# Squares, relu sums and statistics moved between the engines of a planned transformer layer, with a new plan

## The chip, the cores and the metric

The kernel runs on one core of a Trainium2 chip. The metric is the device time of one execution in microseconds (us), the median of three runs. The engines are PE (TensorE: matmuls; PEld is its weight load), DVE (VectorE), ACT (ScalarE), POOL (GpSimd) and SP (SyncE, which here only issues DMAs). PSUM has eight banks of 128x512 fp32, which the kernel hands out by itself.

## The reference, cut to what matters

The input is 4 batches of 1024 tokens with 128 features, all fp32. After a layer norm, two branches read the same normalised rows and are added to the input:

```
xn = layernorm(x)
q, k, v = split(xn @ W_attn + b_attn)             # 16 heads of 8 features
s = q k^T                                         # per head, 1024 x 1024
s = s - mean(s);  s = s / mean(|s|) * gain        # over the whole row, before the mask
r = max(where(causal, s, -1000), 0) ** 4
y = (r / (sum(r) + 1e-6)) @ v;  attn = y @ W_proj + b_proj
ffn = sum over the 2 best of 8 experts: weight * (silu(((xn w1 + b1)(xn w2 + b2)) wg + bg) w3 + b3)
out = x + attn + ffn
```

The attention is no softmax: a score goes through relu and is squared twice, and each row needs the mean of the absolute scores over all 1024 keys, masked or not.

## The kernel before

Everything is one graph of nodes. A node (`add(name, {engine: cost}, emit, deps, take, give, rank, ...)`) is a handful of instructions on one engine, with the buffers that it takes and gives back; where two engines are named, the plan chooses. `Plan.run` is a list scheduler that runs on the host when the program is built: it keeps a model time for each engine, and picks again and again the node that can start first, corrected by the hand-set tables `SOONER` (us by which a kind of node is preferred) and `RANK`. The order that it finds is the program order of each engine's queue, and each queue is in order on the chip. Where the plan sees PE idle inside an open accumulation it adds matmuls with zeros (L1450).

**Attention.** It goes by batch `b` (4) and chunk `c` of 512 queries (2), in `chunk`. Heads are taken four at a time: `r` (0 to 3) is a round, and the four heads of a round lie in four groups of 32 partitions, so that four matmuls of 32 rows or 32 columns run beside each other. Three PE streams run in each chunk:

- *up* (L948): the scores above the diagonal, wanted for mean(|s|) only. Each set fills four banks, and each bank is drained by an absolute sum (`abs`) on DVE (L961) or ACT (L963).
- *score* (L1072): the scores on and under the diagonal, keys in partitions and queries in columns, again four banks for a set. For `c == 1` and each `r` there are four sets `j` = 0 to 3 of 512 columns wholly under the diagonal, and then three on it (`diag`); for `c == 0` only the three. Each bank is made positive into `u1`: the diagonal part by a masked product on DVE (L1091), the rest by ACT (L1098) or DVE (L1100). Then two squares follow, each of two heads at once (up to 1024 columns), `u1` into `u` and `u` into itself, on ACT (L1123) or POOL (L1125).
- *av*: per set a values matmul (L1148, fourth powers against V) and a relu matmul (L1139, the relus against `pick`, one column of ones, which adds up the positive scores of a query; the mean of |s| is made out of that). Both go to one bank `acc` for each `r`.

After the last set of an `r`, `acc` is copied, turned (L1016) and normalised with small DVE and ACT instructions. After four `r`, the chunk's output is turned (L1189), the gate weights are turned (`wT`, L1198), both are projected (L1205, L1207), and DVE adds the result to `xt` (L1214).

**Start.** `norm` makes mean and variance for half a batch at a time: per 128 tokens a `bn_stats` (L473) and a `bn_aggr` (L474), then an addition (L475), a root on ACT (L491), a reciprocal and a product (L479, L480). `route` picks two experts for each token and gives each token and choice a row of `xs` in DRAM; 64 indirect DMAs on POOL (`scatter`, L725), 128 rows each, write the normalised rows there. Each scatter waits for the one before to land.

**Experts.** 36 tiles of 256 rows of `xs` (`experts`) start once the scatters and the weights have landed. Their matmuls (L1276, L1285, L1294) lie between those of the attention, by rank. Each tile ends in two indirect DMAs with addition on POOL (`give`, L1314) into `acc` in DRAM.

**End.** `collect` loads the experts' sums of each batch (L1405) after the last `give`, DVE adds them to `xt` chunk by chunk (L1414), each after the chunk's projection, and SP stores (L1419).

Of the kernel before, what the change touches and what calls it, by code (L numbers as in the profile page):

```python
# [16 lines left out]
P = 128  # L17
# [3 lines left out]
NH = 16  # L21
# [30 lines left out]
class Plan:  # L52
# [3 lines left out]
    HOP = 0.14  # L56
    LAG = {"PE": 0.2, "DVE": 0.085, "ACT": 0.1, "POOL": 0.045}

    SOONER = {"score": 0.41, "v": 0.2, "wT": -0.2, "kappa": -0.03, "gateT": 0.72, "abs": -0.01, "ys": -0.05, "stats": 0.02, "exp": 0.21, "sq": -0.43, "bound": 0.25, "proj": -0.38, "xg": -0.16, "give": 0.82, "yT": -0.45, "sum": 0.42, "heads": -0.15, "gate": -0.76, "headsT": 0.66, "normal": 0.07, "second": -0.74, "relu": 0.04, "y@DVE": 0.58, "relu@DVE": -0.11, "xT": 0.29, "xg@DVE": -0.06, "out": 0.72, "yT@DVE": 0.09, "gate@ACT": 0.47, "g": 0.26, "wT@ACT": 0.52, "mean": -0.26, "sq@ACT": -0.05, "warm": -0.05, "xg@ACT": -0.54, "up": 0.34, "q": -0.02, "blocks": -0.54, "spill": 1.02, "wT@DVE": -0.54, "gain": -0.18, "gates": -0.34, "av": -0.08, "yT@ACT": 0.1, "std": 0.08, "bound@ACT": 1, "scale": 5.03, "heads@ACT": 0.03, "h": 0.26, "q@ACT": -0.52, "reload": 0.77, "sq@POOL": -0.33, "rows": -0.76, "scatter": 0.76, "fill": 1.07, "q@DVE": -0.36, "xT@ACT": -0.2, "absq": 0.1, "hot": 0.31, "bias": -0.05, "turn": -0.03, "abs@ACT": -0.21}
    RANK = {"score": 46, "proj": 1, "yT": -1, "xg": 91, "sums": 10, "h": -28, "tbias": -18, "top": -2, "headsT": -14, "spill": 75, "blocks": 43, "place": 1, "sum": 102, "std": -101, "gateT": -140, "scatter": -43, "xT": -29, "y": -20, "exp": 15, "second": -12, "relu": -6, "mask": 15, "rows": 6, "scale": -200, "turn": -9, "wT": -2, "fill": 8, "ys": -7, "bias": -28, "g": 32, "give": -66, "gate": 22, "absq": 5, "norm": -7, "v": -12, "hot": -41, "stats": 9, "up": 96, "out": -199, "k": 242, "abs": 31, "weight": 33, "reload": 20, "sq": -164, "gain": 149, "kappa": 26, "heads": 17, "mean": 7, "q": -22, "av": 13}  # L60
    MODE = {"up": "rows", "score": "rows", "av": "columns", "gate": "columns", "heads": "columns"}

# [16 lines left out]
    def run(self):  # L79
# [9 lines left out]
        while len(order) < len(self.nodes):  # L89
            best = None  # L90
            for n in ready:
# [11 lines left out]
                for e, took in n.on.items():  # L103
                    s = max(start, at.get(e, 0.0))
                    if e == "PE":
                        s = max(start, at.get(e, 0.0) + self.turn(mode, self.MODE.get(n.name)))
# [10 lines left out]
            if e == "PE":  # L117
                mode = self.MODE.get(n.name)
# [47 lines left out]
def layer_kernel(  # L166
# [63 lines left out]
    def keep(shape, name, dtype=F32):  # L230
# [8 lines left out]
        "yT": (1, [P, CH]), "wT": (1, [P, P]), "asum": (2, [P, 2, CB, NH]), "shead": (2, [P, TB, NH]),  # L239
# [183 lines left out]
    own = keep([E, N_OWN], "own")  # L423
    one8 = keep([P, TB], "one8")
# [36 lines left out]
    def norm(b, rank, begin):  # L461
# [6 lines left out]
        for c in range(NC):  # L468
# [13 lines left out]
            def part(e, i0):  # L482
# [6 lines left out]
            n = add("stats", {"DVE": 1.7}, stats, rank=rank, begin=begin + 0.5 * c)  # L489
            n = add(  # L490
                "std", {"ACT": 0.15}, lambda e, here=here: nc.scalar.activation(s[:, here, 8], s[:, here, 8], AF.Sqrt), deps=[n],  # L491
                rank=rank,
            )
            n = add("std", {"DVE": 0.35}, invert, deps=[n], rank=rank)
# [56 lines left out]
        return cs  # L551

# [5 lines left out]
    def route(rank):  # L558
# [154 lines left out]
        for k in range(2):  # L713
            for b in range(B):
# [7 lines left out]
                for i in range(TB):  # L722
                    def scatter(e, k=k, b=b, i=i):
                        nn = b * TB + i
                        nc.gpsimd.indirect_dma_start(  # L725
                            out=xs, out_offset=bass.IndirectOffsetOnAxis(ap=slot[:, k * NTB + nn : k * NTB + nn + 1], axis=0),
                            in_=of_buf(xn[b])[:, i * WX : (i + 1) * WX], in_offset=None,
                        )

                    prev = add(  # L730
                        "scatter", {"POOL": 1.12}, scatter, deps=[prev, w, filled], rank=rank, after=1.55,
                        give=[xn[b]] if (k, i) == (1, TB - 1) else [],
                    )
                    dones[b].append(prev)
# [748 lines left out]
```

## Time and profile before

| What | us |
|---|---|
| median of 3 runs | 925.73 (922.01 to 926.84) |
| the profiled execution's own time | 921.4 |
| its span, first to last instruction | 919.7 |
| PE busy in the span | 886.8 |
| ACT busy | 808.4 |
| POOL busy | 674.6 |
| DVE busy | 599.5 |

The matmuls of *score* run through the eight chunks in order: batch 0 from 34 to 218 us (its second chunk from 102), batch 1 from 228 to 448, batch 2 from 466 to 696, batch 3 from 697 to 894. The second chunks of batches 1, 2 and 3 take 297 to 448, 542 to 696 and 769 to 894. The scatters run from 80.1 to 275.2 us, and the first expert tile starts at 289.0. All times are of the profiled execution, counted from the start of its span. A busy matmul time counts pipelined matmuls, so it is not work; a set of four matmuls appears as eight records, since each fp32 matmul is two instructions.

### The profile page before, as it was taken

Reading aid. Unit: us, or ns where it says so; the run is one execution under the profiler, and the core shown is the slowest. Engines: PE = TensorE matmul, PEld = TensorE weight load, DVE = VectorE, ACT = ScalarE, POOL = GpSimd, SP = SyncE. Lnnn points to the kernel's source line nnn. Section 1 sums busy time; section 2 is a strip of 40 time slices with the busy share of each in tenths; the row PEclk is TensorE's granted clock in tenths of the full one; section 3 lists DMA queues with packets and bytes.
Section 4 is the critical chain, followed back from the end, with each engine's and each line's share of the span. In section 5 each row is a group of like instructions: output and inputs, shape, how many; then the busy total and the mean of one; then the engine's idle time right before and its main releaser. Section 6 shows DMA issues by size and latency. Waiting matters only on the chain.

```text
span 919.7 us, 22396 instructions
## 1 busy us (share of the span) xinstructions
PE 886.8 (96%) x8013; PEld 479.5 (52%) x8013; DVE 599.5 (65%) x1579; ACT 808.4 (88%) x1925; POOL 674.6 (73%) x469
## 2 busy tenths in 40 slices
PE   7799999999998999999999999999999999999995
PEld 5346533333454655555666656544455566545452
DVE  7798856566786555666566757565567577656555
ACT  5889999999899989889887899799998988899993
POOL 4368888889777868777565773678787776788892
PEclk9799999999999999999999999999999999999998
DMA  4640000000005444553554354433222322232206
GB/s 109 240 155 13 25 22 21 21 25 22 24 22 158 108 118 108 124 136 93 143 136 124 87 132 107 109 76 81 76 71 75 74 66 65 72 80 64 63 9 189
DMA packets 92317, 79.19 MB, mean 86 GB/s; under 512 B 8431, under 2 KB 88366, under 8 KB 92206
## 3 DMA queue, kind: packets, MB, share of 16 engines
q1 hardware_dynamic: 79064, 68.50, 24.6%
q0 software_dynamic: 12416, 8.99, 6.8%
q8 instruction: 63, 1.03, 0.5%
q10 hardware_dynamic: 726, 0.27, 0.1%
q14 instruction: 48, 0.39, 0.1%
HBM read 58.13 MB, written 19.60 MB: 85 GB/s over the span
## 4 chain that ended last, share of the span: by engine, by line
PE 75%; ACT 9%; POOL 7%; DVE 5%; issue 2%; DMA 2%; ACTq 0%; DVEq 0%; POOLq 0%
PE bank L948 14%; PE bank L1072 14%; PE bank L1148 13%; PE bank L1139 8%; PE bank L1285 7%; PE bank L1276 7%; POOL u L1125 5%; PE bank L1294 4%; ACT bank L963 3%; ACT u L1123 3%; ACT u L1098 2%; POOL xs L725 2%; PE bank L1016 2%; PE bank L769 1%; PE bank L825 1%
## 5 line engine op out<-in xcount | busy, mean ns | idle before, releaser
L1125 POOL TENSOR_TENSOR u<-u 128x1024 f32<-128x1024 f32 (+1 forms) x280 | 503.5, 1863 | 125.2 <-ACT u L1098 40.8
L1123 ACT ACTIVATE u<-u 128x1024 f32<-128x1024 f32 (+1 forms) x360 | 339.3, 972 | 8.7 <-POOL u L1125 4.2
L961 DVE TENSOR_REDUCE asum<-bank 128x1 f32<-128x512 f32 (+3 forms) x418 | 205.3, 548 | 56.6 <-PE bank L948 56.1
L1098 ACT ACTIVATE u<-bank 128x512 f32<-128x512 f32 (+2 forms) x375 | 161.7, 498 | 41.0 <-PE bank L1072 24.5
L1072 PE MATMUL bank<-blk,blk 32*128 32x512 f32 (+3 forms) x1536 | 181.4, 527 | 3.9 <-DVE u L1091 2.6
L948 PE MATMUL bank<-blk,blk 32*128 32x512 f32 (+3 forms) x1536 | 184.1, 524 | 0.2
L963 ACT ACTIVATE bank<-bank 128x512 f32<-128x512 f32 (+3 forms) x350 | 169.7, 487 | 15.3 <-PE bank L948 13.2
L1091 DVE SCALAR_TENSOR_TENSOR u<-bank,causal 128x256 f32<-128x256 f32 (+1 forms) x384 | 119.9, 373 | 85.7 <-ACT u L1098 47.8
L1314 POOL DMA_INDIRECT acc<-ye,xg x72 | 113.4, 1576 | 70.7 <-DVE ye L1306 32.5
L1148 PE MATMUL bank<-u,V 128*32 128x512 f32 (+3 forms) x1536 | 162.0, 496 | 1.5 <-POOL u L1125 1.3
L948 PEld LDWEIGHTS bank<-blk,blk 32*128 32x128 f32 x1536 | 93.9, 185 | 75.3 <-DVE asum L961 11.8
L1139 PE MATMUL bank<-u,pick 128*32 128x512 f32 (+3 forms) x1280 | 126.9, 465 | 0.0
L1100 DVE TENSOR_SCALAR u<-bank 128x512 f32<-128x512 f32 (+1 forms) x137 | 87.1, 666 | 50.2 <-PE bank L1072 48.3
L1072 PEld LDWEIGHTS bank<-blk,blk 32*128 32x128 f32 x1536 | 68.9, 184 | 67.3 <-issue 19.7
L1139 PEld LDWEIGHTS bank<-u,pick 128*32 128x32 f32 x1280 | 43.2, 110 | 77.6 <-issue 74.5
L725 POOL DMA_INDIRECT xs<-blk,slot x64 | 63.6, 994 | 26.7 <-DMA xs<-blk,slot 17.7
L1148 PEld LDWEIGHTS bank<-u,V 128*32 128x32 f32 x1536 | 34.2, 108 | 90.7 <-issue 61.1
L1285 PEld LDWEIGHTS bank<-z,w 128*128 128x128 f32 x576 | 67.3, 191 | 19.4 <-DVE z L1360 5.5
L1285 PE MATMUL bank<-z,w 128*128 128x128 f32 x576 | 73.4, 281 | 0.6 <-DVE u L1091 0.6
L1360 DVE SCALAR_TENSOR_TENSOR z<-bank,biases,z 128x128 f32<-128x128 f32 x144 | 43.6, 345 | 42.1 <-ACT z L1353 30.7
L1276 PE MATMUL bank<-xT,w 128*128 128x128 f32 x576 | 70.3, 275 | 0.6 <-ACT u L1098 0.6
L963 ACT ACTIVATION_READ_ACCUMULATOR bank<-bank 128x1 f32 x350 | 68.2, 195 | 0.0
(175 smaller groups left out, 723.5 us busy)
## 6 DMA issues: line engine op xcount, KB each, us to landing
w<-in_L_ffn_w_dram SPq DMA_DIRECT2D x216, 128.0 KB
w<-in_L_ffn_wg_dram SPq DMA_DIRECT2D x72, 256.0 KB
xs<-w SPq DMA_DIRECT2D x1, 4680.0 KB
xg<-xs SPq DMA_DIRECT2D x36, 130.0 KB
acc<-w SPq DMA_DIRECT2D x1, 2048.0 KB
blk<-acc SPq DMA_DIRECT2D x4, 512.0 KB
out_dram<-xt SPq DMA_DIRECT2D x8, 256.0 KB
xt<-in_L_attn_x_dram SPq DMA_DIRECT2D x3, 512.0 KB
```

Of the source, the lines that this page charges most:

```text
L948: nc.tensor.matmul(of_buf(ks_[g])[:, at : at + w], of_buf(q[b])[rows_, ii * P : (ii + 1) * P], of_buf(km[b][r])[rows_, k0 : k0 + w], start ...
L961: nc.vector.tensor_reduce(to, of_, AX.X, ALU.add, apply_absolute_value=True)
L963: nc.scalar.activation(of_, of_, AF.Abs, accum_out=to)
L1072: nc.tensor.matmul(of_buf(ks_[g])[:, at : at + n], of_buf(km[b][r])[rows_, jj * P : (jj + 1) * P], of_buf(q[b])[rows_, c * CH + off : (c + ...
L1091: nc.vector.scalar_tensor_tensor(of_buf(u1)[:, g, :near], of_buf(k)[:, :near], 0.0, allowed[:, :near], ALU.max, ALU.mult)
L1098: nc.scalar.activation(to, s_, AF.Relu)
L1123: nc.scalar.activation(to, s_, AF.Square)
L1125: (nc.vector if e == "DVE" else nc.gpsimd).tensor_tensor(to, s_, s_, ALU.mult)
L1139: nc.tensor.matmul(of_buf(acc)[32 * g : 32 * g + 32, off + lo : CH], pick, of_buf(u1s[g // 2])[:, g % 2, at + lo : at + n], start=begin, s ...
L1148: nc.tensor.matmul(of_buf(acc)[32 * g : 32 * g + 32, off:CH], of_buf(Vb[b])[:, jj, h0 : h0 + 32], of_buf(us[g // 2])[:, g % 2, at : at + n ...
L1276: nc.tensor.matmul(of_buf(k)[:, m * TW + j * TS : m * TW + (j + 1) * TS], weights_of(i, j)[m][:, f * P : (f + 1) * P], of_buf(tile_[i]["xT ...
L1285: nc.tensor.matmul(of_buf(k)[:, g * TW + j * TS : g * TW + (j + 1) * TS], weights_of(i, j)[2][:, f, g * P : (g + 1) * P], of_buf(tile_[i][ ...
```

## The change

Seven things change; the seventh touches everything.

1. For the first batch, the first square of half the heads (`m == 0`, two of the four banks) is no longer made by ACT or POOL out of `u1`. DVE makes it out of the bank itself, max(score, 0) times `u1`, one bank at a time (`sqv`). The bank is given back after that.
2. From the second batch on, for `j` = 1 to 3 of the sets wholly under the diagonal, DVE adds max(score, 0) out of each bank to a sum in SBUF (`more`), starting from the relus of `j == 0`. One relu matmul set for each `r` takes the sum in place of four sets. The bank is given back when both `more` and the relu into `u1` are done.
3. The scatters no longer wait for each other (`apart`); each has a one-element memset on POOL ahead of it.
4. The statistics of batches 1 to 3 are made in one pass (`moments`): `bn_stats` for all 24 blocks of 128 tokens, then six instructions, one root and two instructions for all at once, in place of `bn_aggr` for each block and the rest for each half batch.
5. The gate weights are turned as soon as the chunk before has been projected, not after the chunk's own output was turned, and there are two buffers for them.
6. The experts' sums are added and stored at the end in another order: for the last chunk they are added to `xt` ahead of its projection's addition. The experts' ranks end at 0.93 of the planned span, before at 0.95.
7. The planner's constants are new: `HOP`, `SOONER`, `RANK` (with names of their own for batch 0 and the last chunk), some node costs, and `SPAN` 930 to 895. So the order of all queues is new.

The diff, cut to its core:

```diff
-    HOP = 0.14
+    HOP = 0.12
...
+    def moments(begins, rank):
...
+                for i in range(TB):
+                    nc.vector.bn_stats(stat[:, b, i, 0:6], xt[:, b * TB + i, :])
+            taken.append(add("moments", {"DVE": 2.05}, stats, rank=rank, begin=begins[b - 1]))
...
+        n = add("moments", {"DVE": 0.9}, merge, deps=taken, rank=rank)
+        n = add("moments", {"ACT": 0.15}, lambda e: nc.scalar.activation(v[:, :, 8], v[:, :, 8], AF.Sqrt), deps=[n], rank=rank)
+        return add("moments", {"DVE": 0.35}, invert, deps=[n], rank=rank)
...
+    def apart(d):
+        tc.add_to_no_dep_group("slots", d.ins)
+        tc.declare_no_dep(d.ins, group="slots", reason="no two rows go to one slot")
...
-                        nc.gpsimd.indirect_dma_start(
+                        nc.gpsimd.memset(scrap, 0.0)
+                        d = nc.gpsimd.indirect_dma_start(
...
+                        apart(d)
...
-                        "scatter", {"POOL": 1.12}, scatter, deps=[prev, w, filled], rank=rank, after=1.55,
+                        "scatter", {"POOL": 1.3}, scatter, deps=[prev, w, filled], rank=rank, after=0.3,
...
+        nth = b * NC + c
+            sums, added, relus_0 = [Buf("blk") for _ in range(2)], [], None
+            adds_up = nth >= NC
...
+                    direct = nth < NC and m == 0
...
+                            def product(e, w=w, g=g, k=k, u1=u1, u=u):
+                                nc.vector.scalar_tensor_tensor(
+                                    of_buf(u)[:, g, :w], of_buf(k)[:, :w], 0.0, of_buf(u1)[:, g, :w], ALU.max, ALU.mult
+                                )
+                            squared.append(
+                                add(
+                                    "sqv", {"DVE": t_dve(w)}, product, deps=parts_ + squared, take=[] if squared else [u], give=[k],
+                                    rank=rank - 100, behind=[] if squared else line["sq"],
+                                )
+                            )
...
+                if adds_up and not diag and j:
...
+                            def more(e, m=m, g=g, k=k, first=j == 1, before=relus_0, sums=sums):
+                                to = of_buf(sums[m])[:, g * CH : (g + 1) * CH]
+                                nc.vector.scalar_tensor_tensor(
+                                    to, of_buf(k), 0.0, of_buf(before[m])[:, g, :] if first else to, ALU.max, ALU.add
+                                )
+                            a = add(
+                                "more" + stage, {"DVE": t_dve(CH)}, more, deps=[scores] + (before_ if j == 1 else [added[2 * m + g]]),
...
+                            add("free", {"none": 0.0}, None, deps=[a, e1[2 * m + g]], give=[k])
...
+                    def all_relus(e, sums=sums, acc=acc):
+                        for g in range(4):
+                            nc.tensor.matmul(
+                                of_buf(acc)[32 * g : 32 * g + 32, :], pick, of_buf(sums[g // 2])[:, (g % 2) * CH : (g % 2 + 1) * CH],
+                                start=False, stop=False,
+                            )
+                    relu_job = None
+                    if j == c * CB - 1:
+                        relu_job = dict(acc=acc, emit=lambda e, f=all_relus: f(e), deps=list(added), took=took(CH), give=sums, free=None, last=None, take=[])
...
-        d = add("wT", {"PE": 0.2}, turnw, deps=[weighted[0], a], take=[kw, wT], rank=rank)
+        d = add("wT", {"PE": 0.2}, turnw, deps=[weighted[0]], take=[kw, wT], rank=rank - 15, begin=rank - 30, behind=last_projected)
...
+        final = b == B - 1 and c == NC - 1
+        first = [add_sums(b, c)] if final else []
...
-            deps=[a], give=[ko], rank=rank - 200,
+            deps=[a] + first, give=[ko], rank=rank - 200,
...
-    SPAN, BEGIN = 930.0, 25.0
+    SPAN, BEGIN = 895.0, 25.0
-    F0, F1 = 60.0, BEGIN + SPAN * 0.95
+    F0, F1 = 60.0, BEGIN + SPAN * 0.93
```

## The prediction

> **What bounds the kernel now.** I read the page's busy times first, then a table of stretches cut at the chunks, then the timeline of PE inside one stretch, then the groups by shape, then the waits and the tail.
>
> ```profile
> PE 886.8 (96%) x8013; PEld 479.5 (52%) x8013; DVE 599.5 (65%) x1579; ACT 808.4 (88%) x1925; POOL 674.6 (73%) x469
> ```
>
> Two engines are candidates, PE and ACT; DVE has 320 us free, and the change moves work onto DVE. The shares are means, so I cut them (length, then busy time of PE, PEld, DVE, ACT and POOL, with counts; then clock and DMA):
>
> ```profile
> 102.00:228.00 126.00, 124.14 (x1033) 49.60 (x1037) 80.27 (x189) 118.89 (x244) 112.55 (x85) 1.00 0.07 23
> 297.00:448.00 151.00, 149.97 (x1390) 85.88 (x1390) 89.78 (x233) 136.13 (x313) 109.50 (x64) 1.00 0.47 117
> 542.00:696.00 154.00, 153.83 (x1381) 82.79 (x1385) 94.50 (x235) 138.61 (x332) 109.92 (x65) 1.00 0.36 92
> 769.00:894.00 125.00, 125.00 (x1153) 63.55 (x1149) 75.16 (x190) 115.90 (x265) 103.92 (x60) 1.00 0.25 60
> ```
>
> The first is batch 0's second chunk, before any expert runs: ACT 94% and POOL 89% busy. The other three are the second chunks of batches 1 to 3: PE full, ACT 90%, 90% and 93%, DVE about 60%. The clock is full in all four.
>
> Is PE really full? The Trainium skill ("Perfetto Trace Analysis", Identifying the Most-Contended Engine) says that matmul busy time is no good measure of how near TensorE is to its limit, and tells one to take MFU and the weight-load share instead. The weight load is 52% busy, and by that PE would have room, and matmuls taken away would be worth next to nothing. So I looked at starts instead of busy times, in the second stretch of batch 2 (start, us, line, count):
>
> ```profile
> 662.81 1.14 PE L1072 MATMUL bank<-blk,blk 32*128 32x512 f32 x8
> 663.88 1.07 PE L1148 MATMUL bank<-u,V 128*32 128x512 f32 x8
> 664.77 0.61 PE L1139 MATMUL bank<-u,pick 128*32 128x256 f32 x8
> 665.31 1.15 PE L948 MATMUL bank<-blk,blk 32*128 32x384 f32 x16
> ```
>
> Each set begins when the one before must end: a 512-column set holds PE 0.89 us (663.88 to 664.77) between two sets of column tiles. PE streams without holes; I go with the row, against the rule. In batch 0 PE is only apparently full: the zero matmuls of L1450 fill 11.7 us of the stretch from 102 to 228.
>
> **The change part by part.** Durations:
>
> ```profile
> L1123 ACT ACTIVATE u<-u 128x1024 f32<-128x1024 f32 x284 | 295.5, 1063 | 6.1 <-POOL u L1125 4.0 <-DVE u L1100 0.7 <-DVE u L1091 0.4
> L1125 POOL TENSOR_TENSOR u<-u 128x1024 f32<-128x1024 f32 x228 | 449.3, 2030 | 116.1 <-ACT u L1098 40.8 <-DVE u L1091 37.4 <-DVE u L1100 29.9
> L1091 DVE SCALAR_TENSOR_TENSOR u<-bank,causal 128x256 f32<-128x256 f32 x256 | 91.5, 418 | 48.1 <-PE bank L1072 25.3 <-ACT u L1098 20.0 <-POOL u L1125 2.7
> L1214 DVE TENSOR_TENSOR xt<-bank,xt 128x512 f32<-128x512 f32 x8 | 5.5, 690 | 3.7 <-PE bank L1207 3.6
> ```
>
> *Relus added up.* Three batches, four rounds: four relu sets become one, so 36 sets go. 36 x 0.89 = 32 us of PE, all of it in stretches where PE is full. DVE gains 3 x 4 x 3 sets x 4 banks = 144 instructions with one input in PSUM and one in SBUF, like L1214: 144 x 0.69 = 99 us, 33 in each of the three stretches. Does it fit? Sum of DVE, ACT and POOL, with the 33, over three engines and a stretch shortened by 10.7: first (89.8 + 136.1 + 109.5 + 33) / (3 x 140.3) = 88%; second, the same way, 87%; third 328 / (3 x 114.3) = 96%. The highest such share now is the last stretch's, 79%. The plan can hand relus and absolute sums from ACT to DVE, so 88% I take as possible; 96% not, and I charge 5 us, half of that stretch's gain. In a DVE queue the `more` stand ahead of absolute sums and masks, and for those PE waits, by their banks; see the rivals.
>
> *Squares on DVE in batch 0.* Ten sets for each of four rounds, two banks each: 80 instructions, 64 of 512 columns and 16 of 256: 64 x 0.69 + 16 x 0.418 = 51 us on DVE. Gone are 40 squares, 32 of them of 1024 columns: about 39 us if ACT made them, 74 if POOL did (an estimate from 1.06 and 2.03 us, with 0.63 and 1.13 for the smaller). DVE has 46 us free in 102 to 228 alone. Behind each `sqv` stands whatever DVE does next, and each waits for a relu that may be ACT's.
>
> *Free scatters.* What they can win on POOL:
>
> ```profile
> POOL xs L725 <- DMA xs<-blk,slot: 17.7, 16, 1.9
> ```
>
> That is all: elsewhere POOL puts a square between two scatters (3.07 us from one to the next), and the landing is past by then. Each scatter gains a memset, 0.1 us by the small memsets at the start, and perhaps its own issue gap of 0.17: 64 x 0.1 to 0.27 = 6 to 17 us. So POOL gains 0 to 11 us by this. The experts' first load waits for all 64, so the experts start earlier by what batch 0 gains.
>
> What do these two bring at the end? The experts' matmuls come earlier, but PE is full from 290 on, so only PE time that is now empty in batch 0 counts: about 6 us of idle in 80 to 290, the zero matmuls (12), and 5.5 us idle in 25 to 80. Ends: 0 and 23 us. I take 8, a third, since PE must fit its work between drains there too.
>
> *Statistics.* A `bn_stats` with its `bn_aggr` takes 0.40 us in the start (10.08 to 10.50), alone some 0.29 (an estimate: the first's duration); 24 x 0.11, and eighteen small instructions become eight: about 4.5 us less on DVE before 27 us. Against it, batch 1's normalisation (ACT, 14.2 us) now waits for all three batches' statistics, to about 20. Ends: 4 gained, 4 lost; I take 2 gained, since the reduction for batch 0's bound stands in DVE's queue behind the last of these statistics, at 27.5 us.
>
> *Gate weights, sums, stores.* In DVE's tail the projection's addition waits behind three additions of sums:
>
> ```profile
> 908.39 2.56 DVE L1414 TENSOR_TENSOR xt<-blk,xt 128x512 f32<-128x512 f32 x4 [0.29 <-DMA blk<-acc]
> 911.23 2.02 DVE L1414 TENSOR_TENSOR xt<-blk,xt 128x512 f32<-128x512 f32 x3 [0.28 <-DMA blk<-acc]
> 913.16 0.69 DVE L1214 TENSOR_TENSOR xt<-bank,xt 128x512 f32<-128x512 f32 x1
> 913.88 0.69 DVE L1414 TENSOR_TENSOR xt<-blk,xt 128x512 f32<-128x512 f32 x1
> ```
>
> With the sums ahead, 1.4 us (913.16 less the matmuls' end at about 911.2, less a hop) and the last 0.7 go: 2. The weights' turn leaves the tail: 0.5. SP's stores and the sums' loads still wait for the last `give`; if the experts end late, all of the 2.5 is lost. I take 2.5.
>
> *The new order* has no row. It can cost or win anywhere; the sum holds it at 0, the range at 10 either way.
>
> **Sum**, against the profiled execution's 921.4: 921.4 - 32 + 5 - 8 - 2 - 2.5 = 881.9. The median of the runs shown is 0.47% above that execution (925.73 / 921.4), so 881.9 x 1.0047 = 886.
>
> **Rivals.**
>
> *All of batch 0's slack is won* (0.10): 23 us in place of 8: 871. For it: ACT and POOL carry a quarter less squaring. Against: DVE at 64% there gets 51 us more, and relus before `sqv` are a longer chain.
>
> *ACT, DVE and POOL become the bound in the second chunks* (0.14): if 88% can't be reached either, half to all of the 32 us is lost: 902 to 918, towards the upper end no change. For it: ACT is at 90 to 93% today, and most `more` wait for PE's scores, so DVE's free time isn't all where it is wanted. Against: over the stretches from 297 on, DVE has more free than it is given.
>
> *Banks held too long, slower* (0.08). A bank of scores is now given back after one relu; with ACT and DVE sharing four relus that is about 1.3 us after the scores. With four `more` on DVE the last comes 2.75 us after the scores, 4.1 if DVE makes two relus as well: 1.4 to 2.8 us longer for four of eight banks, one more being `acc`. If PE has nothing that it can do with the three left, each of 36 sets costs that: 50 to 100 us against some 40 gained: 935 to 985. It decides from 1.1 us lost on each set. Against: between two score sets of these stretches lie over 5 us (28 sets in 151 us), and an expert tile's matmuls need two or three banks.
>
> *POOL blocked by DVE.* In the Trainium skill ("SBUF — State Buffer", Who interferes with whom) a DVE instruction with two SBUF inputs shuts out a POOL instruction that reads SBUF. Were the 224 new ones of that kind, up to 150 us of POOL would stall, by an estimate from 0.69 us each, and the result would be slower. Their other input is PSUM; I give it nothing.
>
> **How the numbers follow.** The main case has 0.68, 872 to 900 by its own ends. Half a per cent (921.1 to 930.4) is about what a measurement of this kernel can tell from no change. Faster: 0.68 + 0.10 + 0.10 of the second rival = 0.88; the rest of that rival, 0.04, is no change; slower 0.08. The range, 866 to 914, leaves out the slow rival and the ends of the other two.
>
> **What would show it.** Relu matmul records (L1139's successor) fall by 288 and PE's busy time by over 30 us; `more` is a DVE group of 144 at about 0.69 us, `sqv` of 80; DVE is over 80% busy; the scatters end 15 to 40 us before 275; the tail has the projection's addition last. The argument is wrong if PE has holes in the second chunks that end on DVE instructions (rivals two and three), if `sqv` or `more` take over 0.8 us, or if batch 0's scores still end at 218.

## The result: 2.5% slower

| | before | after |
|---|---|---|
| median | 924.68 us (4 runs) | 947.09 us (945.53 to 951.3, 4 runs) |
| profiled execution, its span | 921.4, 919.7 us | 951.3, 949.6 us |
| mean granted clock | 0.988 | 0.967 |

The ratio is 1.0251 [1.0205, 1.0297]; 886 us were predicted, with a range up to 914. (The 925.73 of the front part is the median of three of the four runs.) Read first what came out as foreseen. From the page of the changed kernel, the busy times, and from its groups the relu sets by four (L1208), the sets that take the sums (L1256), the two forms of `more` (L1230) and `sqv` (L1166):

```profile
PE 892.9 (94%) x7739; PEld 501.3 (53%) x7739; DVE 687.4 (72%) x1677; ACT 788.7 (83%) x1962; POOL 738.7 (78%) x575
...
L1208 PE MATMUL bank<-u,pick 128*32 128x384 f32 (+3 forms) x896 | 73.1, 410 | 0.0
...
L1230 DVE SCALAR_TENSOR_TENSOR blk<-bank,blk 128x512 f32<-128x512 f32 x96 | 60.7, 683 | 14.8 <-ACT u L1147 14.5
L1166 DVE SCALAR_TENSOR_TENSOR u<-bank,u 128x512 f32<-128x512 f32 (+1 forms) x80 | 47.8, 627 | 0.0
...
L1230 DVE SCALAR_TENSOR_TENSOR blk<-bank,u 128x512 f32<-128x512 f32 x48 | 31.0, 686 | 20.8 <-ACT u L1147 18.1 <-PE bank L1119 2.6
...
L1256 PE MATMUL bank<-blk,pick 128*32 128x512 f32 x96 | 12.5, 592 | 0.0
```

The 1280 relu records (126.9 us busy) became 896 + 96 (85.6 us), the 144 additions cost 0.68 us each and the squares 0.69 us or less: the counts and durations of the prediction hold. DVE is 72% busy, not over 80%, and the last scatter starts at 227.9 us instead of 275.2, somewhat more than foreseen. Yet PE's busy time did not fall by 30 us; it rose by 6. Busy time of queued matmuls is not work, as the front part says. The `up` records, before and after:

```profile
L948 PE MATMUL bank<-blk,blk 32*128 32x512 f32 (+3 forms) x1536 | 184.1, 524 | 0.2
```

```profile
L992 PE MATMUL bank<-blk,blk 32*128 32x512 f32 (+3 forms) x1536 | 206.3, 541 | 1.7 <-ACT s L1497 0.7 <-DVE u L1140 0.3 <-ACT u L1147 0.3
```

Their busy time grew by 22 us and that of the `score` records by 18 (181.4 to 199.6), while the mean of one record hardly changed (524 to 541 ns, and 527 to 529). So the same records overlap less. I read this as waiting between the matmuls of a set; no run shows it directly. Where PE waits openly, the chain of releasers names two instructions for which PE had waited 1.8 us in all before (waits: waiting instruction, releaser, sum, times, longest):

```profile
ACT blk L890 <- DVE cstat L842: 22.1, 2, 12.5
...
PE bank L867 <- DVE kapB L849: 14.0, 1, 14.0
...
PE bank L867 <- ACT blk L890: 12.4, 1, 12.4
```

The windows of the changed kernel around these two places, the preparations of batches 2 and 3, with five microseconds out of the first of them ahead (length, busy PE, PEld, DVE, ACT, POOL, then clock), beside one of its second chunks:

```profile
450.00:455.00 5.00, 0.00 (x0) 0.00 (x0) 5.00 (x1) 0.00 (x0) 5.00 (x4) 0.50 0.01 4
...
444.00:464.00 20.00, 5.96 (x32) 2.18 (x26) 18.41 (x13) 4.94 (x10) 14.00 (x8) 0.66 0.10 23
682.00:702.00 20.00, 7.56 (x30) 3.16 (x28) 19.32 (x16) 6.59 (x12) 13.79 (x8) 0.66 0.11 24
...
550.00:682.00 132.00, 130.43 (x1117) 76.72 (x1110) 86.16 (x208) 116.67 (x295) 111.28 (x66) 1.00 0.39 97
```

PE is busy for 6 or 7.6 us in 20, ACT for 5 to 7. Only DVE and POOL are busy throughout, DVE with 13 and 16 instructions, and the granted clock falls to half. The timelines of these two engines at 444 us (start, us, engine, line) show what DVE is busy with:

```profile
444.45 13.57 DVE L841 TENSOR_TENSOR cstat<-cstat 128x1 f32<-128x1 f32 x1
458.06 0.23 DVE L842 TENSOR_SCALAR cstat<-rmask,cstat 128x4 f32<-128x4 f32 x1
```

```profile
444.45 13.55 POOL L1186 TENSOR_TENSOR u<-u 128x1024 f32<-128x1024 f32 x7
```

An addition of two numbers in each partition lasts 13.57 us. It begins with a run of seven squares on POOL and ends with it, to 0.02 us. Before the change the same instruction (L799 there) took 0.147 to 0.152 us in all four batches. It stood once more at 683.0, for 12.81 us. The code of this part was not changed. What changed is the order: it puts seven squares in a row on POOL just there (more on such rows in 5).

### The profile page after: what moved, and what is told of

It is laid out like the page before. It is cut to its first block, busy times and chain, and to the rows that moved or that the text cites. A ratio compares the mean times of both kernels' runs of the same rounds, so it can differ in the third digit from the quotient of the medians.

```text
span 949.6 us, 22138 instructions
## 1 busy us (share of the span) xinstructions
PE 892.9 (94%) x7739; PEld 501.3 (53%) x7739; DVE 687.4 (72%) x1677; ACT 788.7 (83%) x1962; POOL 738.7 (78%) x575
## 5 line engine op out<-in xcount | busy, mean ns | idle before, releaser
L1186 POOL TENSOR_TENSOR u<-u 128x1024 f32<-128x1024 f32 (+1 forms) x322 | 571.2, 1907 | 116.5 <-ACT u L1147 29.9
L1184 ACT ACTIVATE u<-u 128x1024 f32<-128x1024 f32 (+1 forms) x278 | 268.3, 994 | 7.8 <-DVE u L1140 2.8
L1147 ACT ACTIVATE u<-bank 128x512 f32<-128x512 f32 (+2 forms) x448 | 200.0, 520 | 63.3 <-PE bank L1119 30.9
L1005 DVE TENSOR_REDUCE asum<-bank 128x1 f32<-128x512 f32 (+3 forms) x386 | 190.8, 549 | 48.2 <-PE bank L992 47.1
L992 PE MATMUL bank<-blk,blk 32*128 32x512 f32 (+3 forms) x1536 | 206.3, 541 | 1.7 <-ACT s L1497 0.7
L1007 ACT ACTIVATE bank<-bank 128x512 f32<-128x512 f32 (+3 forms) x382 | 185.8, 490 | 19.8 <-PE bank L992 16.7
L1119 PE MATMUL bank<-blk,blk 32*128 32x512 f32 (+3 forms) x1536 | 199.6, 529 | 2.4 <-DVE u L1140 0.8
L992 PEld LDWEIGHTS bank<-blk,blk 32*128 32x128 f32 x1536 | 110.6, 190 | 75.8 <-ACT u L1147 11.0
L1119 PEld LDWEIGHTS bank<-blk,blk 32*128 32x128 f32 x1536 | 80.1, 184 | 68.1 <-issue 17.3
L1208 PE MATMUL bank<-u,pick 128*32 128x384 f32 (+3 forms) x896 | 73.1, 410 | 0.0
L1230 DVE SCALAR_TENSOR_TENSOR blk<-bank,blk 128x512 f32<-128x512 f32 x96 | 60.7, 683 | 14.8 <-ACT u L1147 14.5
L1387 PEld LDWEIGHTS bank<-xT,w 128*128 128x128 f32 x576 | 67.2, 192 | 0.8 <-DVE asum L1005 0.8
```

The lines of the kernel that those rows point to most:

```text
L992: nc.tensor.matmul(of_buf(ks_[g])[:, at : at + w], of_buf(q[b])[rows_, ii * P : (ii + 1) * P], of_buf(km[b][r])[rows_, k0 : k0 + w], start ...
L1005: nc.vector.tensor_reduce(to, of_, AX.X, ALU.add, apply_absolute_value=True)
L1007: nc.scalar.activation(of_, of_, AF.Abs, accum_out=to)
L1119: nc.tensor.matmul(of_buf(ks_[g])[:, at : at + n], of_buf(km[b][r])[rows_, jj * P : (jj + 1) * P], of_buf(q[b])[rows_, c * CH + off : (c + ...
L1147: nc.scalar.activation(to, s_, AF.Relu)
L1184: nc.scalar.activation(to, s_, AF.Square)
```

## The experiments

All ratios are to the kernel before, run on the same chip. The medians of the kernel before lay between 924.5 and 926.3 us. The edits are to the changed kernel where nothing else is said. A kernel called "replanned" has a new order of all queues; the others keep theirs.

**1. The form of the small addition.** Two SBUF inputs against one, and the same edit in the kernel before as a control.

```diff
-            nc.vector.tensor_tensor(mean, ks[:, 0:1], ks[:, 1:2], ALU.add)
+            nc.vector.tensor_reduce(mean, ks, AX.X, ALU.add)
```

> The changed kernel, with the mean of the keys (the 128x1 addition of two SBUF columns on DVE that took 13.6 and 12.8 us at 444 and 683) written as a reduction over the two columns, with one SBUF input. Nothing else changes, and all queues keep their order. Theory A, POOL's squares shut that addition out until POOL runs dry, and PE waits 14 and 12 us for what hangs on it: both stalls go, with the half clock after them; 947 falls by 25 to 42 us, to 905 to 922, and the reduction takes under 0.3 us. Theory B, banks are held too long by the additions out of PSUM and the preparation comes late for want of buffers: the holes at 446 to 460 and 686 to 698 stay, 940 to 950. Theory C, the three engines beside PE are overloaded in the second chunks: 935 to 948, since a hole is only the place where a backlog shows.

> The kernel before, with the same reduction in place of the addition, as a control. In its trace the addition took 0.15 us in all four places, so theory A, B and C all expect no change: 922 to 928. If it becomes faster, the reduction helps in some way other than by the stall.

Measured: 946.82 us, 1.0231 [1.0214, 1.0248], and 925.75, 0.9989 [0.9972, 1.0006]. No gain. The timelines of DVE and of POOL in the edited kernel say why:

```profile
439.67 13.54 DVE L842 TENSOR_SCALAR cstat<-rmask,cstat 128x4 f32<-128x4 f32 x1
```

```profile
439.62 13.55 POOL L1186 TENSOR_TENSOR u<-u 128x1024 f32<-128x1024 f32 x7
```

The reduction passed; the next instruction of the queue, a product with a scalar that takes 0.23 us elsewhere, stood in its place, and again at 678.5 for 12.85 us, also until the squares ended. So the shut-out is not bound to two SBUF inputs: a second form, SBUF to SBUF with a scalar from SBUF, is caught too.

**2. The three small instructions on ACT.** Order kept, in the changed kernel and, as a control, in the kernel before.

```diff
-            nc.vector.tensor_tensor(mean, ks[:, 0:1], ks[:, 1:2], ALU.add)
-            nc.vector.tensor_scalar(nkm, rmask, mean, -1.0 / T, ALU.mult, ALU.mult)
+            nc.scalar.activation(mean, ks[:, 0:1], AF.Identity, bias=ks[:, 1:2])
+            nc.scalar.activation(nkm, rneg, AF.Copy, scale=mean)
...
-            nc.vector.tensor_scalar(kapB[b % 2], same, kab, sign, ALU.mult, ALU.mult)
+            nc.scalar.activation(kapB[b % 2], signed, AF.Copy, scale=kab)
```

> The changed kernel, with all three instructions of the preparation that stood waiting on DVE taken to ACT, in the same places of the program: the addition of the two columns, the product with the row mask, and the 128x128 product for the bound (its sign multiplied in once at the start). With only the addition rewritten, the next instruction, the product with the row mask, stood 13.5 and 12.9 us in its place. Theory A (POOL's back-to-back squares shut out DVE instructions of some forms on SBUF): no form of that kind is left in the preparation; both holes of PE and the half clock after them go: 905 to 922. Theory D (DVE is held there by something else that lies behind these instructions, a semaphore or POOL's data): whatever stands there next waits as long, 940 to 950.

> The kernel before with the same three instructions on ACT. There the 128x128 product stood 1.6 to 2.0 us once, the others never. Theory A: gain of 0 to 3 us, or a loss of as much where ACT waits for DVE's reduction: 921 to 929. Theory D says the same.

Measured: 923.25 us, 0.9982 [0.9966, 0.9999], and 923.45, 0.9982 [0.9972, 0.9992]. The changed kernel gains 24 us, the kernel before 0.2%. ACT takes 0.29 to 0.41 us for each of them, and no stall is left. So the two stalls are the whole loss of the change, and without them it is no faster than before: of the forecast gain of 39 us some 38 are still missing. The rest of the runs look for those, from the changed kernel with this edit on, here called the kernel of 2.

**3. What the additions are worth.** No `more`, every relu set on PE; replanned. Once with the edit of 1, once with that of 2.

```diff
-            adds_up = nth >= NC
+            adds_up = False
```

> The changed kernel with the reduction, and without the relus added up by DVE: the 36 relu matmul sets are back on PE and 144 DVE instructions go; the plan is made anew with the same tables. Against the same kernel with them: if the additions won their 32 us of PE in part, this is 15 to 32 us slower (theory A, which leaves that step of the prediction alone). If they cost by held banks or DVE load (theories B and C), this is as fast or faster by up to 20 us.

> The changed kernel with those three on ACT and without the relus added up by DVE; the 36 relu matmul sets are back on PE. With the reduction alone this version took 935.2 with 7.3 us of a stall left. If the additions win their PE time once no stall is in the way: 12 to 32 us slower than with them. If they win nothing since ACT, POOL and DVE are the bound there: within 8 us.

Measured: 935.2 us, 1.0106 [1.0087, 1.0125], and 929.27, 1.0046 [1.0033, 1.0058]. The first run still has a stall of its own (7.35 us), so the second is the one to read. Against 923.25 the additions seem to bring 6 us of the predicted 27, but not where they were to bring them. From the last score of batch 0 to the last score of all, where the second chunks lie, it takes 673.0 us with the additions (231.1 to 904.1) and 674.7 without (229.7 to 904.4). Behind the last score, where no addition runs, it takes 17.5 us with them and 23.0 without, a difference between the two orders. So the additions win about 2 us.

**4. Why so little.** The prediction counted DVE's time and, as a rival, the bank that is held longer. The timelines of ACT and DVE in the kernel of 2 show a third thing, how the relu and the addition of the same four banks lie:

```profile
353.54 2.06 ACT L1151 ACTIVATE u<-bank 128x512 f32<-128x512 f32 x4 [1.20 <-PE bank L1123]
```

```profile
354.18 2.48 DVE L1234 SCALAR_TENSOR_TENSOR blk<-bank,blk 128x512 f32<-128x512 f32 x4 [1.19 <-ACT u L1151]
```

Both read the bank and neither needs the other's result. Yet DVE, idle for 1.19 us, begins only when the first relu has ended, 0.64 us after its start, and the waits name ACT:

```profile
DVE blk L1230 <- ACT u L1147: 32.7, 38, 2.1
...
ACT u L1147 <- DVE blk L1230: 12.9, 18, 1.0
```

(These two lines are of the changed kernel; each engine waits for the other.) In this program two engines do not read one bank at once: one waits for the other's semaphore. So a bank is held for relu plus addition, 0.64 + 0.68 us here, where the two were thought to run side by side. Two runs in the same order shorten either half. In the first the additions make 64 of 512 columns; in the second the relus of these banks do, and the squares read what the buffers held before. Both leave out that work, and their times are read for the holding alone.

```diff
-                                    to, of_buf(k), 0.0, of_buf(before[m])[:, g, :] if first else to, ALU.max, ALU.add
+                                    to[:, :64], of_buf(k)[:, :64], 0.0, of_buf(before[m])[:, g, :64] if first else to[:, :64], ALU.max, ALU.add
```

> The kernel with the three instructions on ACT (923.3), each of the 144 additions of relus cut to 64 of its 512 columns and emitted in the same place, so that all queues keep their order; the sums of relus left out are wrong by that. In that kernel the second chunks of batches 1 to 3 run 6 us each behind the order's own times, without the additions they don't. Theory E: two engines read one bank after the other (the addition on DVE waits for the relu on ACT of the same bank, in 38 places for 32.7 us), so each bank of scores is held by relu plus addition; a short addition frees the bank 0.5 us sooner: 10 to 25 us faster, 898 to 913. Theory F: DVE has too much to do: faster by as much, for its load falls by 75 us. Theory G: the loss lies elsewhere (sums, acc, the one late relu matmul): within 5 us.

```diff
+                        def relu(..., part_=bool(adds_up and j and not diag)):
-                            s_, to = of_buf(k)[:, near:w], of_buf(u1)[:, g, near:w]
+                            e_ = near + 64 if part_ else w
+                            s_, to = of_buf(k)[:, near:e_], of_buf(u1)[:, g, near:e_]
```

> The same kernel with full additions, and the relus of the same 144 banks cut to 64 columns, again in the same order; the squares behind them read stale columns. Theory E (bank held by relu, then addition): the bank comes free 0.4 us sooner and DVE waits less for ACT: 8 to 25 us faster. Theory F (DVE's own load): DVE's work does not change: within 5 us, or a little more from the relus that DVE makes itself. Theory G: within 5 us.

Measured: 911.54 us, 0.9854 [0.9833, 0.9875], and 912.15, 0.9867 [0.9847, 0.9888]. In the first, the second chunks of batches 1 to 3 take 151.0, 148.7 and 128.3 us, against 158.5, 155.8 and 134.3 in the kernel of 2: 20.6 us less. In the second it is 19 less. The chunk of batch 1 as windows, of the kernel of 2, of the first run and of the second, with the same 1290 matmul records:

```profile
306.00:464.50 158.50, 153.56 (x1290) 88.28 (x1290) 103.07 (x246) 140.04 (x348) 137.49 (x79) 1.00 0.38 91
```

```profile
315.70:466.70 151.00, 148.77 (x1290) 86.58 (x1290) 83.77 (x246) 139.51 (x347) 137.40 (x79) 1.00 0.39 95
```

```profile
314.50:466.80 152.30, 149.78 (x1290) 87.40 (x1290) 102.56 (x246) 123.52 (x348) 137.19 (x79) 1.00 0.39 94
```

The first run relieves DVE (103.1 to 83.8 us) and leaves ACT as it was; the second relieves ACT (140.0 to 123.5) and leaves DVE. Both gain nearly the same, so neither engine's load explains both gains; the bank, which both runs free sooner, explains them. Since both leave work out, the 20 us are an upper bound for the holding alone. With the bank freed sooner, the stretch from the last score of batch 0 to the last of all takes 652.3 and 653.5 us, against 676.1 before and 673.0 in the kernel of 2. So most of the predicted 27 us is there once the bank is free.

In both runs batch 0 ended later than in the kernel of 2 (scores to 240.8 instead of 231.1 in the first, to 239.6 in the second), although nothing there was edited. I have no cause for that; it hides part of the gain in the whole time.

**5. Free the bank, pay in SBUF.** The additions that follow the relu of their bank in the program (100 of 144) read the relu in SBUF; order kept. This frees the bank early with the work left whole, and is the way that the change did not take.

```diff
-                                    to, of_buf(k), 0.0, ...
+                                    to, of_buf(u1s[m])[:, g, :] if (id(u1s[m]), g) in made else of_buf(k), 0.0, ...
```

> The kernel with the three small instructions on ACT (923.25) in its own order; the additions that follow the relu of their bank in the program read that relu from SBUF instead of the bank, so the bank is free after the relu alone. If the bank held through relu and addition one behind the other is what costs some 19 us of the second chunks: 904 to 912. If the load of the additions on VectorE is what costs: no change, 920 to 926. These additions have two SBUF inputs, as the small addition that stood for 13.57 us beside GpSimd's squares: if such inputs are shut out by each square, an addition waits for the next gap of GpSimd, the sums come late, and it is slower than 930.

Measured: 1048.3 us, 1.1346 [1.1308, 1.1383], 125 us slower than without the edit. Its groups, additions from SBUF, squares on POOL, and the additions still from PSUM:

```profile
L1192 POOL TENSOR_TENSOR u<-u 128x1024 f32<-128x1024 f32 (+1 forms) x322 | 582.3, 1925 | 145.0 <-ACT u L1153 38.4 <-ACT u L1190 30.3 <-DVE u L1145 29.5
...
L1236 DVE SCALAR_TENSOR_TENSOR blk<-u,blk 128x512 f32<-128x512 f32 x71 | 125.1, 1809 | 15.2 <-ACT u L1153 15.2
L1236 DVE SCALAR_TENSOR_TENSOR blk<-u,u 128x512 f32<-128x512 f32 x29 | 52.3, 1810 | 16.5 <-ACT u L1153 16.5
...
L1236 DVE SCALAR_TENSOR_TENSOR blk<-bank,blk 128x512 f32<-128x512 f32 x25 | 15.8, 678 | 0.6 <-PE bank L1124 0.6
```

With two SBUF inputs the addition takes 1.81 us in the mean, with one 0.68. The mean hides two kinds. The same two groups by their shortest, median and longest, in ns:

```profile
L1236 DVE SCALAR_TENSOR_TENSOR blk<-u,blk x71: 674/693/14484, 313.1 to 1007.0; 128x512 f32<-128x512 f32 x71
L1236 DVE SCALAR_TENSOR_TENSOR blk<-u,u x29: 674/1270/7465, 307.2 to 1000.7; 128x512 f32<-128x512 f32 x29
```

At least half of the larger group run at full speed, and a few stand for up to 14.48 us; the 100 lose 113 us together. How long one stands depends on the squares beside it. Two rows of seven squares of this run, and the row of the changed kernel at 444 us, with the shortest, median and longest square and the starts of the first and last:

```profile
L1192 POOL TENSOR_TENSOR u<-u x7: 1888/2336/2337, 306.2 to 319.5; 128x1024 f32<-128x1024 f32 x7
```

```profile
L1192 POOL TENSOR_TENSOR u<-u x7: 2446/2466/2487, 484.4 to 495.5; 128x1024 f32<-128x1024 f32 x7
```

```profile
L1186 POOL TENSOR_TENSOR u<-u x7: 2443/2463/2486, 444.5 to 455.6; 128x1024 f32<-128x1024 f32 x7
```

In the first row no record overlaps the next. An addition gets in after each of the first six squares, having waited for one at most, and the squares from the second on take 2.34 us instead of 1.89. In the other two a square starts every 1.85 us but is recorded with 2.44 to 2.49, so that each begins before the one before has ended. There DVE gets nothing in: one addition stood 14.48 us to the end of the second row. Beside squares recorded with 2.40 us or less no addition of this run took over 2.41 us. All seven rows that held a DVE instruction for 10 us or more, in the changed kernel, in that of 1 and in this one, begin before the record of an indirect DMA on POOL has ended. Whether that makes the second kind was not tried. Both kinds say why an input in PSUM was a sound choice.

**6. Squares on DVE in batch 0.** First without them (replanned, with the edit of 1 and with that of 2), then only in the second chunk (replanned), then in the same order with 64 columns, where the second square reads the relus, so that the first square is left out there, on every engine.

```diff
-                    direct = nth < NC and m == 0
+                    direct = False
```

> The changed kernel with the reduction, and without the squares out of PSUM in batch 0: 40 squares are back on ACT and POOL. Batch 0's scores ended at 231 us in the changed kernel and at 218 before, so the squares on DVE may have cost 12 us rather than won 8. If they do: 5 to 15 us faster than with them. If they win and the loss in batch 0 has another cause (the new order, DVE's queue): 5 to 20 us slower, and scores of batch 0 end later than 231.

> The changed kernel with those three on ACT and without the squares out of PSUM in batch 0. With the reduction alone it took 961.7, with stalls of 3.0 and 9.2 us left and additions of sums at the end that took 2.4 us in place of 0.7. If these squares win time of their own: 10 to 35 us slower than with them. If what it lost is the stalls and the end: within 8 us.

```diff
-                    direct = nth < NC and m == 0
+                    direct = nth == 1 and m == 0
```

> The kernel with the three on ACT, and the squares out of PSUM only in batch 0's second chunk, planned anew with the same tables. DVE is 92% busy from 31 to 85 us there, with the routing and the preparation, and ACT only 64% from 55 to 85. If those first squares on DVE are what makes batch 0 late: its scores end before 222 in place of 231, and the whole by -10 to +5 us, as the order behind is another. If batch 0's lateness is the order itself: the end of its scores stays at 228 to 234.

```diff
-                                    of_buf(u)[:, g, :w], of_buf(k)[:, :w], 0.0, of_buf(u1)[:, g, :w], ALU.max, ALU.mult
+                                    of_buf(u)[:, g, :64], of_buf(k)[:, :64], 0.0, of_buf(u1)[:, g, :64], ALU.max, ALU.mult
...
-                        lambda e, ...: square(e, w, u, u), deps=a
+                        lambda e, ...: square(e, w, u1 if direct else u, u), deps=a
```

> The kernel with the three small instructions on ACT (923.25) in its own order; the squares on VectorE in batch 0 make 64 columns, and the second square of these heads reads the relus, so that the first square is left out of the result there. If VectorE's load by these squares (and the bank held through them) is what makes batch 0 end 13 us later than in the kernel before: batch 0's scores end at 218 to 222 in place of 231, whole kernel 911 to 916. If it is the new order or the statistics, nothing: 921 to 925.

Measured: 961.69 us, 1.0378 [1.0357, 1.0399]; 944.4, 1.0204 [1.0168, 1.024]; 939.25, 1.0161 [1.014, 1.0181]; and 918.58, 0.9933 [0.9907, 0.9959]. The three replanned kernels can't be read for the squares. In the third, batch 0's scores do end earlier, at 220.3 instead of 231.1, and yet the whole is 16 us longer, all behind batch 0, where nothing was edited but the order. The last run keeps the order: with the load of the squares gone, batch 0's scores end at 226.9 and the kernel gains 4.7 us. So the work itself costs batch 0 about 4 us. What the squares would cost there on ACT and POOL, in the same order, was not tried, so the worth of moving them stays open. The other 8.5 of the 12.7 by which its scores end later than before (231.1 against 218.4) come with the new order. The start of batch 0, before and then in the changed kernel:

```profile
31.00:102.00 71.00, 67.08 (x593) 36.16 (x595) 58.84 (x156) 61.64 (x153) 49.67 (x37) 0.94 0.33 121
```

```profile
31.00:102.00 71.00, 64.62 (x532) 38.34 (x530) 64.87 (x165) 55.06 (x136) 45.43 (x52) 0.90 0.35 129
```

Fewer matmuls, squares and ACT instructions lie in the same 71 us, the clock is lower, and DVE is 91% busy. Here it is short of time; the mean of 65% hid it.

**7. The scatters.** Waiting again, in the new order; and free, in the old order (an edit to the kernel before).

```diff
-                        apart(d)
```

> The kernel with the three on ACT, the scatters waiting for each other again, the memsets kept, the same order. In the changed kernel groups of two to eight scatters follow each other 1.3 us apart; each would then wait for the landing, about 2.3 us: some 40 such pairs by 1.0 to 1.3 us are 40 to 50 us of POOL in 72 to 228. If POOL is on the path of batch 0: 10 to 40 us slower. If scatters have room (theory of the prediction: 0 to 11 us on POOL): 0 to 8 us slower.

```diff
+                        nc.gpsimd.memset(scrap, 0.0)
-                        nc.gpsimd.indirect_dma_start(
+                        d = nc.gpsimd.indirect_dma_start(
...
+                        apart(d)
```

> The kernel before in its own order, with one edit: the scatters do not wait for each other and each has the one-element memset ahead of it. The prediction gave this part 0 to 11 us on GpSimd, which was idle 17.7 us for it: 914 to 926. If the 32 us that the same waits cost in the changed order were its worth in any order, it is 895 to 905. If the 64 memsets and scatters that run closer together hold up other work of GpSimd, 927 or more.

Measured: 953.49 us, 1.0316 [1.0282, 1.0349], and 916.79, 0.9919 [0.9891, 0.9948]. In the new order the waits cost 30 us, in the old one 7.7. The waits of POOL in the first run, and the scatter group of the second:

```profile
POOL xs L769 <- DMA xs<-blk,slot: 52.6, 34, 2.5
```

```profile
L733 POOL DMA_INDIRECT xs<-blk,slot x64 | 63.6, 994 | 11.8 <-issue 9.9 <-POOL scrap L732 1.6 <-PE bank L1157 0.3
```

The new order puts scatters close behind each other, so there the landing is waited for 34 times instead of 16, and batch 0's scores end at 261.0 instead of 231.1. The price of a wait belongs to an order. The second run is the fastest kernel of this study with the work left whole, 0.8% ahead of the kernel before, by one edit of the seven and no new plan. (The run of 8, which has the same edit and ran on another chip, is 0.4% ahead.)

**8. The tail.** The last sums ahead of the projection's addition, on top of the free scatters of 7 (before_free); old order up to the last microseconds.

```diff
+        first = [add_sums(b, c)] if final else []
...
-            deps=[a], give=[ko], rank=rank - 200,
+            deps=[a] + first, give=[ko], rank=rank - 200,
```

> before_free (916.79) with the sixth part of the change alone: the experts' sums of the last chunk are added ahead of its projection's addition, the experts' ranks left at 0.95; the order is the old one up to the last microseconds. The prediction gave this end 2.5 us: 913 to 916. If the 7.7 us by which the changed kernel's end is shorter come from it: 908 to 911. If they come from the order in which the last experts lie between the last scores, and not from the sums: 916 to 918, no change.

Measured: 922.49 us, 0.9962 [0.995, 0.9974]. From the last score to the end it takes 25.4 us, with 25.3 in before_free and 25.2 before: the order of the sums alone wins nothing. The 7.7 us that the changed kernel's tail is shorter (17.5 us) come from elsewhere in the new order of the last work; which part of it was not tried. Nor is it known why this run lies 0.4% above before_free. So the free scatters are worth 0.4 to 0.8% in the old order. The statistics, the gate weights and the planner's constants were not run alone.

## Why the prediction was wrong

Stretch by stretch, in us of the profiled executions, with the difference to before:

| | before | predicted | kernel of 2, no stalls | additions cut to 64 columns (4) |
|---|---|---|---|---|
| to the last score of batch 0 | 218.4 | -10 | 231.1 (+12.7) | 240.8 |
| from there to the last score | 676.1 | -27 | 673.0 (-3.1) | 652.3 (-23.8) |
| behind it | 25.2 | -2.5 | 17.5 (-7.7) | 17.5 |

The changed kernel adds its two stalls, 24 us, to the kernel of 2. (Of the 10 us predicted in the first row, 8 are for squares and scatters and could also be won in the second.)

**Relus added up: -32 and 5 back, measured -2 to -3.** The count (288 records gone) and the additions' duration held. The step that failed is the fit: the three engines' busy times were added up (88%) as if a relu and an addition could lie beside each other. They exclude each other at the bank, and about 20 us of the second chunks went there (4). The Trainium skill ("PSUM — Partial Sum Buffer", PSUM bank collisions raise a hardware error) says that two engines must be kept apart at a bank by semaphores, since the chip does not hold one back. The 32.7 and 12.9 us of waits are that discipline in the trace. Rival three had the right place, banks held too long. Its size was off: it asked for 1.4 to 2.8 us lost at each of 36 sets and called 1.1 the point of decision. Measured is 20.6 / 36 = 0.57 at most, so alone it would have left a small gain.

**POOL blocked by DVE: 0, measured +24.** This step made the kernel slower where it would have been the same. The prediction asked whether the 224 *new* instructions could shut out POOL. It had the wrong set and the wrong direction: old instructions, with all operands in SBUF and 0.15 and 0.23 us long, were shut out *by* POOL, and only the new order brought them beside such a row of squares. The rule of the Trainium skill ("SBUF — State Buffer", Who interferes with whom) was at hand. It names two SBUF inputs as a case, and `tensor_scalar` as an operation that can enter it, and says that who issues first keeps the ports for the whole instruction. The traces agree on both forms (L841, and L842 in run 1) and differs on the length: by the rule a loser waits out one square, 1.9 us; here it waited out seven, 13.6 us. Run 5 shows both, the wait for one square and the wait for all seven, and what goes with each; why was not tried. The rest is a chain: ACT's keys and PE's bound wait for DVE's number, no score can start, and the granted clock falls to half (0.66 in the mean of each 20 us).

**Squares and scatters: -8, measured +12.7 in batch 0.** The scatters alone won 3.8 to 7.7 us in the old order (8, 7), within the 0 to 11 that they were given on POOL. The squares were placed by DVE's mean load, and batch 0's start has none to give (6): their work costs about 4 us there. The other 8.5 us came with the new order.

**Statistics: -2; tail: -2.5, measured -7.7.** The scores begin at 31.4 us in the kernel of 2 and at 34.1 before, which fits the first, but no run isolates it. That the tail shrank was luck: the named cause wins nothing (8).

**The new order: 0, range 10 either way.** It is no single term. It brought the stalls (24 us), the 8.5 us of batch 0 and the shorter tail, and it set the price of the scatters' waits (30 us against 7.7). Terms measured in different orders do not add up, and what in the order makes batch 0 late stays open. The three replanned kernels of 6 agree in kind: an edit inside batch 0 costs 15 to 21 us against its own starting point (946.82 or 923.25) after a new plan with tables set for another graph.

## What to carry to other kernels

Before an operation is given to a second engine, look at what the two share besides time: here they shared the PSUM bank, and free DVE time bought 2 or 3 us where 27 were expected. After any change of order, list the instructions whose duration has grown against their own kind; a 0.15 us instruction that lasts 13.6 us is seen at once in the minimum and maximum of its tile, and in no busy share. And try each part of a large change alone in the old order: here one part of seven won 0.4 to 0.8%, while the whole lost 2.5%.

## What was not expected of the hardware

A run of POOL squares kept a DVE instruction with SBUF operands waiting to its very end: 13.57 us for seven squares, 12.81 us in the next batch, 10.8 us beside five. There POOL pays nothing visible: a square starts every 1.85 us. But not every row of squares does this. Where the records of the squares did not overlap (5), DVE got in after six of seven, and POOL slowed down too, from 1.89 to 2.34 us a square. A pause of POOL lets DVE in too. Before the change a single square stood at the same place, with nothing behind it on POOL until 694.71 us, and the addition ran right after its end at 688.80 (timelines of DVE and POOL of the kernel before):

```profile
688.81 0.15 DVE L799 TENSOR_TENSOR cstat<-cstat 128x1 f32<-128x1 f32 x1
```

```profile
686.32 2.48 POOL L1125 TENSOR_TENSOR u<-u 128x1024 f32<-128x1024 f32 x1
```

Not every small instruction is caught: a `tensor_scalar` of one column (L806) ran in its 0.15 us at 688.36, inside that square.
